# Perceiver block on one core: buffers and loads of the output weights, the order of a split product, and the columns of a score row

## The chip, the cores and the metric

The kernel runs on one core of a Trainium2 chip. The metric is the device time of one execution in microseconds (us); lower is better. TensorE (PE in the profile, with PEld for its weight loads) does the matmuls, VectorE (DVE), ScalarE (ACT) and GpSimd (POOL) the element-wise work, and every DMA of this kernel is issued by SyncE (SP). A partition is one of the 128 rows of the on-chip memory.

## The reference, cut to what matters

There are 8 batches with 64 query rows of width 512 and a context of 1601 rows of width 512. Five blocks follow each other, each on a layer norm and with a residual:

```python
x = x + xattn0(ln(x), ctx)   # 32 heads of 128, 8 key/value heads; Wq, Wkv, Wo with biases
x = x + mamba(ln(x))         # 1024 channels, 16 states, 64 steps: conv, silu, softplus, scan, gate, W_out
x = x + ffn0(ln(x))          # ternary 512 x 512 weight and a bias
x = x + xattn1(ln(x), ctx)   # softmax(x ctx^T) ctx, no weights
x = x + attn1(ln(x))         # causal, 32 heads of 16, rotary; wq, wk, wv, wo
x = x + ffn1(ln(x))          # octonion ternary, gated: 512 -> 1360 -> 512
```

Here `ln` is the layer norm. Everything is fp32, and the result is wanted nearly at fp32. The rest of the names below follow this list: "the main attention" is xattn0, which is most of the arithmetic, and "the second cross attention" is xattn1.

## The kernel before, in words

**Two streams.** The main attention is one stream, `x_all` (L517): 64 units, one for each batch and key/value head, and in each unit six steps that interleave the keys (L363), values (L334), scores (L385), the products with the values (L464) and, for each odd batch, the output product with Wo (`x_wo`, L492 to 515, into the tile `w_ps`, added at L514). The other five blocks are "side chains", one for each pair of batches (a group; groups 0 to 3 are batches 0-1, 2-3, 4-5 and 6-7). A side chain (L761) can begin when both its batches have their rows of xattn0; it is a generator that goes through `mamba` (L789), `ffn`, `xattn1` (L997), `attn1` (L1106) and `ffn1`. Two more generators run at the beginning: `halves` (L606) and `prep` (L620, which makes the ternary weights).

**What sets the order.** `run` (L1285) takes one piece of the main stream after the other, and after each piece lets the side generators go on until they have yielded the cost that is due by then (`advance`, L1314; the goal is linear from a chain's start over its SPAN, L1367: 3.1 main batches for groups 0 and 1, 2.6 for group 2). In this way the program is written in one order. The instructions of the side chains on VectorE, ScalarE and GpSimd are kept in that order (L55 to 76, `keep_in_program_order`); those of TensorE and the DMA issues of SyncE are placed by the scheduler, which lays all engines out on a time line and takes a buffer when it is free. So a side chain that waits for a buffer on that line is placed later, and so are the pinned pieces behind it.

**The tail.** Behind the last unit the main stream is flushed (the rest of the last unit and its Wo product). Then the pools of the main stream are closed, new ones with other sizes opened (L47, `BUFS_TAIL`), the pinning is off, and group 3's chain goes through in the form for the tail (`tail=True`): weights as pairs of 4 KB a partition, 12 buffers for `w2`. What is left of group 2's chain is interleaved behind it and takes the tags w2 and b4 from the tail's pool (REST, L1374: 8 and 3 buffers).

**Precise products.** Where fp32 accuracy is wanted at the faster fp32r rate, a number is split into a high part that fp32r holds exactly and a low part, the rest. A product is then three matmuls, high by high, high by low and low by high (`mm3`, L742). `halves` makes the two parts of Wo (32 tiles of 128 x 512), W_outT (8 tiles) and the four matrices of attn1 (16 tiles) once, in the beginning, and stores them to DRAM (`wo_s`, `wout_s`, `wat_s`): it loads a tile (L614), splits it by a ScalarE copy and a GpSimd subtraction (L616, L105 and 106), and stores both parts (L617). It uses the tag `wo` with three buffers, the same that `x_wo` uses later for its weights (L507).

**Buffers of the change.** A tag is a ring of buffers, and L46 (`BUFS`) gives their number before the tail. `lv` holds tiles of 4 KB a partition, three of them: u (L793), dt (L847) and dus = dt times u (L865) of the mamba block. `w2` holds tiles of 2 KB, three of them: the weights of every `mm3` outside the tail, so that the two parts of a weight take two buffers and come in two DMAs (L753 to 755). W_out is read in `mamba_out` (L968), which splits the gated output and calls `mm3` once for each of eight chunks; this comes behind the scan of all chunks (L949 to 952), and the gates (L958, with projections at L801) stand between. The keys' weights of the main stream have a tag of their own, `wk`, with one buffer; `wo` is as large.

**The second cross attention.** For each of the two batches, `scores` (L1005) loads ctxT in pieces of up to 256 columns (L1018), multiplies (L1021: the row of 512 is split over two halves of the array, so four matmuls a piece), adds the halves (L1032, L1034), and takes the maximum, the exponential and the sum by tiles. Outside the tail the 1601 columns lie in three tiles S of 512, 512 and 577 columns; the third is filled from two accumulators, 384 and 194 columns. `values` (L1051) transposes the weights in 13 blocks (L1059), loads ctxN (L1072, L1074) and multiplies (L1077).

Of the kernel before, what the change touches and what calls it, by code (L numbers as in the profile page):

```python
# [16 lines left out]
P = 128  # L17
# [28 lines left out]
BUFS = {"a2": 5, "lv": 3, "bc": 1, "xpad": 1, "b2": 5, "b4": 2, "w2": 3, "xr": 2}  # L46
# [32 lines left out]
class Kernel:  # L79
# [412 lines left out]
    def x_wo(self, b, i):  # L492
# [13 lines left out]
        for g in range(G):  # L506
            w = self.sb("wo", [P, 2, D], FR, pool=self.xp, bufs=WOB)  # L507
            nc.sync.dma_start(out=w.bitcast(FP), in_=self.wo_s[i][:, g])
            parts = ((0, 0), (0, 1), (1, 0))
            for a, m in parts:  # L510
                nc.tensor.matmul(ps, lhsT=ot[:, a, g].rearrange("p b t -> p (b t)"), rhs=w[:, m], start=k == 0, stop=k == len(parts) * G - 1)  # L511
                k += 1
            yield 0.64
# [92 lines left out]
    def halves(self):  # L606

        nc, i = self.nc, self.i
        todo = [(i["Wo"][k * G + g], self.wo_s[k][:, g]) for k in range(NKV) for g in range(G)]
        todo += [(i["W_outT"][h], self.wout_s[h]) for h in range(NCH)]  # L610
        todo += [(i["attnT"][m, c], self.wat_s[m][c]) for m in range(4) for c in range(NC)]
        for src, dst in todo:
            t = self.sb("wo", [P, 2, D], FR, pool=self.xp, bufs=WOB)
            nc.sync.dma_start(out=t[:, 1].bitcast(FP), in_=src)  # L614
            yield 0.5
            self.split(t[:, 0], t[:, 1], t[:, 1].bitcast(FP), eng=nc.gpsimd)  # L616
            nc.sync.dma_start(out=dst, in_=t.bitcast(FP))  # L617
            yield 0.5
# [123 lines left out]
    def mm3(self, ps, lhsT, wt, N, start, stop, exact=False, tg="w2"):  # L742
# [5 lines left out]
        elif self.tail:  # L748
# [7 lines left out]
        nc.tensor.matmul(ps, lhsT=lhsT(0), rhs=wh, start=start, stop=False)  # L756
        if not exact:
            nc.tensor.matmul(ps, lhsT=lhsT(0), rhs=wl, start=False, stop=False)
        nc.tensor.matmul(ps, lhsT=lhsT(1), rhs=wh, start=False, stop=stop)  # L759
# [29 lines left out]
    def mamba(self, gi, x, xo):  # L789
# [3 lines left out]
        u = self.sb(self.tv, [P, NCH, 2, T])  # L793
# [174 lines left out]
    def mamba_out(self, c, uc, ps):  # L968
        yt = self.sb("a2", [P, 2, P], FR)
        self.split(yt[:, 0, :], yt[:, 1, :], uc.rearrange("p b t -> p (b t)"))  # L970
        self.mm3(ps, lambda a: yt[:, a, :], self.wout_s[c], D, c == 0, c == NCH - 1, tg=self.t4)
# [25 lines left out]
    def xattn1(self, bs, x, xo):  # L997
# [3 lines left out]
        GW = [(0, (256, 256)), (1, (256, 256)), (2, (192, 192)), (2, (194,))]  # L1001
        SW = [512, 512, 577]
        TS = ((0, 4), (4, 8), (8, NT))

        def scores(k, b):  # L1005
            q0 = k * T
            if self.tail:
                s = self.sb("bc", [T, LP])
                S = [s[:, :512], s[:, 512:1024], s[:, 1024:]]
            else:  # L1010
                S = [self.sb("b2", [T, 512]), self.sb("b2", [T, 512]), self.sb("b2", [T, 578])]
# [26 lines left out]
            nm = self.sb("s1m", [T, 4])  # L1038
            for m in range(3):
                nc.vector.tensor_reduce(nm[:, m : m + 1], S[m][:, : SW[m]], AX.X, ALU.max)  # L1040
            nc.vector.tensor_reduce(nm[:, 3:4], nm[:, 0:3], AX.X, ALU.max, negate=True)
            sm2 = self.sb("s1s", [T, 4])
            for m in range(3):
                nc.scalar.activation(S[m][:, : SW[m]], S[m][:, : SW[m]], AF.Exp, bias=nm[:, 3:4], accum_out=sm2[:, m : m + 1])
            sm = sm2[:, 3:4]
            nc.vector.tensor_reduce(sm, sm2[:, 0:3], AX.X, ALU.add)
# [4 lines left out]
        def values(k, b, S, sm):  # L1051
            q0 = k * T
            pts = []
            for m, (t0, t1) in enumerate(TS):
                pt = self.sb("b2", [P, 5, T])
                tp = self.acc().rearrange("p (t q) -> p t q", q=T)
                for t in range(t0, t1):
                    r = rows_of(t)
                    nc.tensor.transpose(tp[:r, t - t0, :], S[m][:, (t - t0) * P : (t - t0) * P + r], self.ident[:T, :T])  # L1059
# [312 lines left out]
MAMBA_TAGS = ("a2", "lv", "bc", "xpad", "sm")  # L1372
# [117 lines left out]
```

## Time and profile before

| what | value |
|---|---|
| runs | 2690.39, 2688.52 and 2685.12 us; median 2688.52 |
| the profiled execution | 2687.19 us |
| span of its profile (first to last instruction on the core) | 2685.1 us |
| mean granted clock of TensorE over the span | 0.983 |
| matmul records | 16,320 |
| DMA issues on SyncE | 1,331 |
| bytes moved | 466 MB, 174 GB/s over the span |
| last add of the main attention (`w_ps`, L514) begins | 2385.5 us |

Times in the views below are microseconds from the start of the span, and "busy" is the time in which an engine executed instructions. The table by stretches gives for each engine the busy time and, in brackets, the number of instructions in the stretch, then the clock that TensorE was granted (1.00 is full speed), the mean busy share of the sixteen DMA engines, and what they moved. The same table can be made for the instructions of one line alone; the first figure pair is then PE and the second PEld. The view of waits gives, for an engine, what it was about to do, what ended its wait, and the total, number and longest of these waits in us.

When the blocks of the groups ran in this execution (us):

| group | mamba | xattn1 | attn1 | ffn1 |
|---|---|---|---|---|
| 0 | 671-1125 | 1137-1268 | 1338-1425 | 1495-1577 |
| 1 | 1218, gates to 1734 | 1792-1922 | 1970-2094 | 2153-2232 |
| 2 | 1870-2375 | 2402-2510 | from 2539 | to 2650 |
| 3 (in the tail) | 2388-2532 | 2547-2592 | 2597-2645 | to 2685 |

### The profile page before, as it was taken

The page shows a single profiled execution, that of the slowest core. Times are in us where ns is not written, and L with a number is a line of the kernel's source. Part 1 is how long each engine was busy: PE and PEld are TensorE (multiplying, and loading weights), DVE is VectorE, ACT ScalarE, POOL GpSimd, SP SyncE. Part 2 cuts the span into 40 slices and gives each one's busy share as a digit, 9 for nine tenths or more (in the row PEclk, how much of TensorE's full clock was granted, in tenths as well). Part 3 has the DMA queues.
Part 4 walks back from the last instruction along what each step waited for, and adds up shares of the span by engine and source line. Part 5 has one row for each costly group of instructions (what it writes and reads, how often), then busy time and mean ns, then how long its engine had stood idle before and what let it go on. Part 6 is the DMA issues. An engine that isn't in the chain of part 4 may idle for free.

```text
span 2685.1 us, 43976 instructions
## 1 busy us (share of the span) xinstructions
PE 2549.7 (95%) x16320; PEld 2269.3 (85%) x16320; DVE 1667.6 (62%) x2739; ACT 1350.2 (50%) x3128; POOL 1247.6 (46%) x1243
## 2 busy tenths in 40 slices
PE   7999999999999999999999999999999999977797
PEld 6988999999999899978989988988898898964544
DVE  4534357665687775545567676554657777668754
ACT  4545454344556554544555554544546545436433
POOL 2434463463368663521367457521239556405420
PEclk9999999999999999999999999999999999987899
DMA  9788876675213244764324452665343455466674
GB/s 308 225 295 276 281 239 190 203 240 180 67 66 105 68 133 150 232 190 145 97 98 148 149 161 89 216 201 164 102 135 92 137 159 155 143 226 216 234 261 166
DMA packets 311126, 466.08 MB, mean 174 GB/s; under 512 B 88440, under 2 KB 187768, under 8 KB 306432
## 3 DMA queue, kind: packets, MB, share of 16 engines
q1 hardware_dynamic: 310912, 463.28, 53.4%
q8 instruction: 128, 2.10, 0.3%
q14 instruction: 86, 0.70, 0.1%
HBM read 389.66 MB, written 73.53 MB: 173 GB/s over the span
## 4 chain that ended last, share of the span: by engine, by line
PE 68%; DMA 9%; DVE 9%; POOL 7%; issue 4%; ACT 3%; SPq 0%; POOLq 0%; DVEq 0%; ACTq 0%
PE v_ps L334 16%; PE k_ps L363 16%; PE o_ps L464 10%; PE s_ps L385 8%; POOL a L65 3%; PE w_ps L511 2%; PE acc L274 2%; DVE a L65 2%; PE acc L1077 2%; PE acc L801 2%; PE acc L1021 1%; PE acc L759 1%; PE acc L756 1%; POOL ss L452 1%; DMA b<-in_ctxT_dram 1%
## 5 line engine op out<-in xcount | busy, mean ns | idle before, releaser
L363 PE MATMUL k_ps<-cxb,wk 128*128 128x384 f32 x2304 | 470.3, 347 | 35.3 <-DVE mx L392 13.2
L334 PE MATMUL v_ps<-wv,cxb 128*128 128x256 f32 x3456 | 467.9, 281 | 1.0 <-DVE kt L109 0.6
L334 PEld LDWEIGHTS v_ps<-wv,cxb 128*128 128x128 f32 x3456 | 438.0, 188 | 19.3 <-issue 11.7
L363 PEld LDWEIGHTS k_ps<-cxb,wk 128*128 128x128 f32 x2304 | 405.3, 191 | 53.2 <-DVE mx L392 15.6
L464 PE MATMUL o_ps<-S,v 128*128 128x256 f32 (+1 forms) x1664 | 413.6, 381 | 7.4 <-DVE rw L479 4.0
L385 PE MATMUL s_ps<-q,kt 128*128 128x256 f32 (+1 forms) x2496 | 413.7, 299 | 5.2 <-DVE mx L392 2.4
L385 PEld LDWEIGHTS s_ps<-q,kt 128*128 128x128 f32 (+1 forms) x2496 | 342.8, 185 | 28.5 <-issue 6.9
L388 ACT COPY S<-s_ps 128x512 f32<-128x512 f32 (+1 forms) x448 | 241.9, 553 | 241.0 <-PE s_ps L385 236.6
L452 POOL TENSOR_TENSOR ss<-ss,S 128x512 f32<-128x512 f32 x254 | 349.3, 1375 | 14.7 <-ACT S L427 1.3
L392 DVE TENSOR_TENSOR mx<-s_ps,mx 128x512 f32<-128x512 f32 x256 | 175.1, 684 | 264.0 <-ACT S L388 262.7
L464 PEld LDWEIGHTS o_ps<-S,v 128*128 128x128 f32 (+1 forms) x1664 | 298.6, 190 | 46.7 <-issue 5.2
L429 POOL TENSOR_TENSOR ss<-S,S 128x512 f32<-128x512 f32 x64 | 84.5, 1320 | 469.4 <-ACT S L427 469.1
L108 ACT ACTIVATE kt<-k_ps,c_bk 128x384 fp32r<-128x384 f32 (+1 forms) x256 | 152.0, 594 | 246.9 <-PE k_ps L363 245.9
L426 DVE TENSOR_TENSOR S<-S,m_ps 128x512 f32<-128x512 f32 (+1 forms) x448 | 257.3, 640 | 20.5 <-PE m_ps L412 20.2
L427 ACT ACTIVATE S<-S 128x512 f32<-128x512 f32 (+1 forms) x448 | 246.7, 599 | 43.4 <-DVE S L426 42.7
L109 DVE SCALAR_TENSOR_TENSOR kt<-k_ps,c_bk,kt 128x384 fp32r<-128x384 f32 (+1 forms) x256 | 160.9, 629 | 158.0 <-ACT kt L108 156.5
L337 ACT COPY v<-v_ps 128x256 f32<-128x256 f32 (+1 forms) x416 | 152.5, 368 | 198.4 <-PE v_ps L334 196.0
L334 PE MATMUL v_ps<-wv,cxt 128*128 128x256 f32 (+1 forms) x1536 | 206.5, 282 | 1.5 <-DVE mx L392 1.0
L334 PEld LDWEIGHTS v_ps<-wv,cxt 128*128 128x128 f32 (+1 forms) x1536 | 192.7, 175 | 10.5 <-issue 3.4
L65 DVE TENSOR_TENSOR_SCAN a<-a,a 128x512 f32<-128x512 f32 x96 | 154.7, 1613 | 62.9 <-POOL a L65 62.8
L363 PE MATMUL k_ps<-cxt,wk 128*128 128x450 f32 x768 | 178.6, 375 | 1.4 <-DVE mx L392 1.3
L65 POOL TENSOR_TENSOR a<-a,bc 128x512 f32<-128x512 f32 x96 | 128.1, 1335 | 90.7 <-DVE a L65 90.7
(357 smaller groups left out, 3947.8 us busy)
## 6 DMA issues: line engine op xcount, KB each, us to landing
wo<-d_wo SPq DMA_DIRECT2D x128, 512.0 KB, 5.3
wk<-d_wk SPq DMA_DIRECT2D x63, 512.0 KB, 3.5
wv<-d_wv SPq DMA_DIRECT2D x31, 1024.0 KB, 5.7
cst<-in_ctxT_dram SPq DMA_DIRECT2D x96, 192.0 KB, 3.0
b<-in_ctxN_dram SPq DMA_DIRECT2D x36, 512.0 KB, 3.7
d_q<-q_t SPq DMA_DIRECT2D x32, 512.0 KB, 5.9
q<-d_q SPq DMA_DIRECT2D x64, 256.0 KB, 3.1
d_wo<-wo SPq DMA_DIRECT2D x32, 512.0 KB, 5.7
```

The costliest lines, as they stand in the source:

```text
L65: return lambda *a, **k: self.tc.keep_in_program_order(f(*a, **k))
L109: eng.scalar_tensor_tensor(lo, src, bias, hi.bitcast(FP), ALU.add, ALU.subtract)
L334: nc.tensor.matmul(ps[:r], lhsT=cx[:, a, c, o : o + r], rhs=w[:, m, c, :], start=k == 0, stop=k == 11)
L337: nc.scalar.copy(vt[:r], ps[:r])
L363: nc.tensor.matmul(ps[:, :wd], lhsT=w[:, a, c, :], rhs=cx[:, m, c, :], start=k == 0, stop=k == 11)
L385: nc.tensor.matmul(sp[:r, gi, :], lhsT=kt[:, a, o : o + r], rhs=q[:, m, :], start=k == 0, stop=k == 2)
L388: nc.scalar.copy(s[:r, :n], sp[:r, :n])
L392: nc.vector.tensor_tensor(mx, sp, S[0] if len(S) == 1 else mx, ALU.max)
L426: nc.vector.tensor_tensor(sv, sv, ps[:r, 1:2].to_broadcast([r, w, 256]), ALU.add)
L427: nc.scalar.activation(sv, sv, AF.Exp, scale=ISC)
L452: nc.gpsimd.tensor_tensor(ss, ss, S[n], ALU.add)
L464: nc.tensor.matmul(ps[:, 0], lhsT=self.v[(b, j, t)][:r, hc : hc + P], rhs=S[t // 2][:r, t % 2], start=t == 0, stop=t == NT - 1)
```

## The change

Six edits, all outside the form of the tail except the third:

1. `lv` has two buffers and not three, and u gets a tag of its own, `lu`, with one: the same room in other rings. `w2` has four buffers and not three (2 KB a partition more).
2. `mamba_out` outside the tail loads the two parts of a W_out chunk as one tile of 4 KB a partition (512 KB in one DMA) from the tag `lv`, where dt and dus lay, and no longer as two from `w2`. That is 24 DMAs fewer in the three groups (1331 to 1307).
3. `mm3` multiplies high by high, low activation by high weight, high activation by low weight; the last two were the other way round.
4. `halves` has two loads ahead of the split, and issues the load of tile k+2 behind the store of tile k.
5. `scores` outside the tail lays the 1601 columns out as 512, 512, 512 and 66 (65 of them used), each from one accumulator; the small tile has a tag `s1x`. Each batch so has one more maximum and one more exponential.
6. The very last quarter of Wo (batch 7, head 7, g = 3) is loaded into the tag `wk`, and not into the fourth use of a ring of three.

```diff
--- before.py
+++ after.py
@@ -43,7 +43,7 @@
 CPLAN = (0, 1, 2, None, None, 3)
 AVPLAN = ((), (), (0, 1, 2, 3), (4, 5, 6, 7), (8, 9, 10, 11), (12,))
 EXPLAN = ((0,), (1, 2), (3,), (4, 5), (6,), ())
-BUFS = {"a2": 5, "lv": 3, "bc": 1, "xpad": 1, "b2": 5, "b4": 2, "w2": 3, "xr": 2}
+BUFS = {"a2": 5, "lv": 2, "lu": 1, "bc": 1, "xpad": 1, "b2": 5, "b4": 2, "w2": 4, "xr": 2}
 BUFS_TAIL = {"a2": 6, "du": 2, "bc": 2, "xpad": 4, "s4": 11, "kb": 3, "b2": 8, "b4": 3, "w2": 12, "xr": 2}
 
 
@@ -504,7 +504,8 @@
         ps = self.px.tile([P, D], FP, name=self.nm("w_ps"), tag="kv", bufs=KVB)
         k = 0
         for g in range(G):
-            w = self.sb("wo", [P, 2, D], FR, pool=self.xp, bufs=WOB)
+            last = (b, i, g) == (self.B - 1, NKV - 1, WOB)
+            w = self.sb("wk" if last else "wo", [P, 2, D], FR, pool=self.xp, bufs=1 if last else WOB)
             nc.sync.dma_start(out=w.bitcast(FP), in_=self.wo_s[i][:, g])
             parts = ((0, 0), (0, 1), (1, 0))
             for a, m in parts:
@@ -609,12 +610,22 @@
         todo = [(i["Wo"][k * G + g], self.wo_s[k][:, g]) for k in range(NKV) for g in range(G)]
         todo += [(i["W_outT"][h], self.wout_s[h]) for h in range(NCH)]
         todo += [(i["attnT"][m, c], self.wat_s[m][c]) for m in range(4) for c in range(NC)]
-        for src, dst in todo:
-            t = self.sb("wo", [P, 2, D], FR, pool=self.xp, bufs=WOB)
-            nc.sync.dma_start(out=t[:, 1].bitcast(FP), in_=src)
+        ts = {}
+
+        def load(k):
+            if k < len(todo):
+                ts[k] = self.sb("wo", [P, 2, D], FR, pool=self.xp, bufs=WOB)
+                nc.sync.dma_start(out=ts[k][:, 1].bitcast(FP), in_=todo[k][0])
+
+        load(0)
+        load(1)
+        yield 1
+        for k, (src, dst) in enumerate(todo):
+            t = ts.pop(k)
+            self.split(t[:, 0], t[:, 1], t[:, 1].bitcast(FP), eng=nc.gpsimd)
             yield 0.5
-            self.split(t[:, 0], t[:, 1], t[:, 1].bitcast(FP), eng=nc.gpsimd)
             nc.sync.dma_start(out=dst, in_=t.bitcast(FP))
+            load(k + 2)
             yield 0.5
 
     def prep(self):
@@ -739,13 +750,13 @@
         self.nc.sync.dma_start(out=w, in_=wt)
         self.nc.tensor.matmul(ps, lhsT=x, rhs=w, start=start, stop=stop)
 
-    def mm3(self, ps, lhsT, wt, N, start, stop, exact=False, tg="w2"):
+    def mm3(self, ps, lhsT, wt, N, start, stop, exact=False, tg="w2", pair=False):
 
         nc = self.nc
         if exact:
             wh = self.sb(tg, [P, D], FR)[:, :N]
             nc.sync.dma_start(out=wh.bitcast(FP), in_=wt)
-        elif self.tail:
+        elif self.tail or pair:
             w = self.sb(tg, [P, 2, D], FR)
             nc.sync.dma_start(out=w.bitcast(FP), in_=wt)
             wh, wl = w[:, 0], w[:, 1]
@@ -754,9 +765,9 @@
             nc.sync.dma_start(out=wh.bitcast(FP), in_=wt[:, 0])
             nc.sync.dma_start(out=wl.bitcast(FP), in_=wt[:, 1])
         nc.tensor.matmul(ps, lhsT=lhsT(0), rhs=wh, start=start, stop=False)
+        nc.tensor.matmul(ps, lhsT=lhsT(1), rhs=wh, start=False, stop=stop and exact)
         if not exact:
-            nc.tensor.matmul(ps, lhsT=lhsT(0), rhs=wl, start=False, stop=False)
-        nc.tensor.matmul(ps, lhsT=lhsT(1), rhs=wh, start=False, stop=stop)
+            nc.tensor.matmul(ps, lhsT=lhsT(0), rhs=wl, start=False, stop=stop)
 
     def chain(self, gi, bs):
         nc, i = self.nc, self.i
@@ -790,7 +801,7 @@
         nc, i = self.nc, self.i
         tail = self.tail
         lt = self.lnT(x, P, hl=False, tg="a2")
-        u = self.sb(self.tv, [P, NCH, 2, T])
+        u = self.sb(self.tv if tail else "lu", [P, NCH, 2, T])
         gs = 2 if tail else 4
 
         def proj(m):
@@ -968,7 +979,7 @@
     def mamba_out(self, c, uc, ps):
         yt = self.sb("a2", [P, 2, P], FR)
         self.split(yt[:, 0, :], yt[:, 1, :], uc.rearrange("p b t -> p (b t)"))
-        self.mm3(ps, lambda a: yt[:, a, :], self.wout_s[c], D, c == 0, c == NCH - 1, tg=self.t4)
+        self.mm3(ps, lambda a: yt[:, a, :], self.wout_s[c], D, c == 0, c == NCH - 1, tg=self.tv if not self.tail else self.t4, pair=True)
 
     def softplus(self, x, shape, eng):
 
@@ -998,8 +1009,13 @@
 
         nc, i = self.nc, self.i
         lt = self.lnT(x, P, hl=False)
-        GW = [(0, (256, 256)), (1, (256, 256)), (2, (192, 192)), (2, (194,))]
-        SW = [512, 512, 577]
+        if self.tail:
+            GW = [(0, (256, 256)), (1, (256, 256)), (2, (192, 192)), (2, (194,))]
+            SW = [512, 512, 577]
+        else:
+            GW = [(0, (256, 256)), (1, (256, 256)), (2, (256, 256)), (3, (66,))]
+            SW = [512, 512, 512, 65]
+        NS = len(SW)
         TS = ((0, 4), (4, 8), (8, NT))
 
         def scores(k, b):
@@ -1008,7 +1024,7 @@
                 s = self.sb("bc", [T, LP])
                 S = [s[:, :512], s[:, 512:1024], s[:, 1024:]]
             else:
-                S = [self.sb("b2", [T, 512]), self.sb("b2", [T, 512]), self.sb("b2", [T, 578])]
+                S = [*(self.sb("b2", [T, 512]) for _ in range(3)), self.sb("s1x", [T, 66], bufs=1)]
             o = 0
             for m, ws in GW:
                 ps = self.acc()
@@ -1035,15 +1051,15 @@
                 o += e
                 if not self.tail:
                     yield 2 * len(ws)
-            nm = self.sb("s1m", [T, 4])
-            for m in range(3):
+            nm = self.sb("s1m", [T, 5])
+            for m in range(NS):
                 nc.vector.tensor_reduce(nm[:, m : m + 1], S[m][:, : SW[m]], AX.X, ALU.max)
-            nc.vector.tensor_reduce(nm[:, 3:4], nm[:, 0:3], AX.X, ALU.max, negate=True)
-            sm2 = self.sb("s1s", [T, 4])
-            for m in range(3):
-                nc.scalar.activation(S[m][:, : SW[m]], S[m][:, : SW[m]], AF.Exp, bias=nm[:, 3:4], accum_out=sm2[:, m : m + 1])
-            sm = sm2[:, 3:4]
-            nc.vector.tensor_reduce(sm, sm2[:, 0:3], AX.X, ALU.add)
+            nc.vector.tensor_reduce(nm[:, 4:5], nm[:, 0:NS], AX.X, ALU.max, negate=True)
+            sm2 = self.sb("s1s", [T, 5])
+            for m in range(NS):
+                nc.scalar.activation(S[m][:, : SW[m]], S[m][:, : SW[m]], AF.Exp, bias=nm[:, 4:5], accum_out=sm2[:, m : m + 1])
+            sm = sm2[:, 4:5]
+            nc.vector.tensor_reduce(sm, sm2[:, 0:NS], AX.X, ALU.add)
             nc.vector.reciprocal(sm, sm)
             yield 3
             return S, sm
@@ -1056,7 +1072,8 @@
                 tp = self.acc().rearrange("p (t q) -> p t q", q=T)
                 for t in range(t0, t1):
                     r = rows_of(t)
-                    nc.tensor.transpose(tp[:r, t - t0, :], S[m][:, (t - t0) * P : (t - t0) * P + r], self.ident[:T, :T])
+                    src = S[3][:, :r] if t == 12 and len(S) > 3 else S[m][:, (t - t0) * P : (t - t0) * P + r]
+                    nc.tensor.transpose(tp[:r, t - t0, :], src, self.ident[:T, :T])
                 e = min(t1, 12) - t0
                 nc.scalar.copy(pt[:, :e, :], tp[:, :e, :])
                 if t1 == NT:
@@ -1369,7 +1386,7 @@
 HALVES_START = 0.1
 HALVES_END = 0.97
 HALVES_COST = 56.0
-MAMBA_TAGS = ("a2", "lv", "bc", "xpad", "sm")
+MAMBA_TAGS = ("a2", "lv", "lu", "bc", "xpad", "sm")
 FFN_TAIL = (("l", 0), ("l", 1), ("a", 0), ("l", 2), ("a", 1), ("d", 0), ("a", 2), ("d", 1), ("d", 2))
 REST = {"w2":8,"b4":3}
 OTB = 1
```

`self.tv` is `lv` outside the tail and `s4` in it, `self.t4` is `w2` and `s4`.

## The prediction

> **What bounds the kernel now.** I read the page's totals first, then a table of five stretches that I cut at visible marks: the attention; its flush; and the three parts of the tail, split where the last group's scan begins (2441 us, first L941) and ends (2530 us).
>
> ```profile
> PE 2549.7 (95%) x16320; PEld 2269.3 (85%) x16320; DVE 1667.6 (62%) x2739; ACT 1350.2 (50%) x3128; POOL 1247.6 (46%) x1243
> ...
> core 0: us, PE busy (x) PEld busy (x) DVE busy (x) ACT busy (x) POOL busy (x), PEclk, DMA share, GB/s
> 67.00:2345.00 2278.00, 2226.55 (x14556) 2047.17 (x14556) 1415.77 (x2281) 1163.77 (x2668) 1134.48 (x1118) 1.00 0.51 162
> 2345.00:2385.00 40.00, 33.00 (x172) 27.40 (x171) 23.42 (x48) 14.44 (x33) 5.26 (x7) 0.96 0.54 173
> 2385.00:2441.00 56.00, 38.98 (x251) 30.54 (x249) 34.62 (x101) 30.02 (x91) 2.44 (x11) 0.75 0.87 292
> 2441.00:2530.00 89.00, 68.62 (x396) 46.61 (x394) 82.78 (x113) 52.95 (x157) 61.57 (x61) 0.85 0.54 178
> 2530.00:2686.00 156.00, 131.48 (x683) 74.36 (x683) 78.50 (x155) 56.77 (x124) 24.54 (x25) 0.96 0.67 233
> ```
>
> Up to 2345 us TensorE is busy 2226.55 of 2278 us: whatever matmul is put there lengthens it, and only 51.5 us could be won. The tail is another regime: part A (56 us) has DMA at 0.87 and a clock of 0.75; part B (89 us) has VectorE busy 82.78 us, 93%, so the scan sets it; part C (156 us) has TensorE at 84%. Next, who TensorE waits for. The weights that the change is about are small entries:
>
> ```profile
> PE k_ps L363 <- DMA wk<-d_wk: 9.2, 5, 4.1
> ...
> PE acc L758 <- DMA w<-d_wout: 3.2, 2, 2.2
> ...
> PE w_ps L511 <- DMA wo<-d_wo: 3.0, 4, 1.2
> ...
> PE acc L758 <- DMA w<-d_wat: 1.7, 2, 1.0
> ```
>
> The columns are us in total, times, longest: 17.1 us in all; no more than that can come from the weights' waits directly.
>
> **What the change does to the order.** The two programs' instruction orders, laid side by side, show the moves. The main attention's 12,496 matmuls are the same. The side chain of group 2 (batches 4 and 5) stands about 540 main matmuls earlier by its gate (L801); group 1's is 220 to 580 earlier from its gate on; group 0's up to its gate is unmoved. I read this as a queue effect: side work is in program order on VectorE, ScalarE and GpSimd, so a chain that waits for a w2 tile holds back the next chain's scan; with a fourth tile and 4 KB W_out pairs it holds it less. What counts is the end: before, group 2's feed-forward block and whole second cross attention stand behind the last main matmul; after, 119 of these matmuls stand ahead of it (56 of L1021, 25 of L1077, 26 of L1059, 8 exact ones, 4 of L709). The tail begins with group 2's self-attention.
>
> **Part by part.** *Attention: +33.* The moved matmuls cost what the same lines cost in the attention (each fp32 L1021 and L1077 matmul is two records):
>
> ```profile
> 67.00:2345.00 2278.00, 27.38 (x224) 13.76 (x224) 1.00 0.51 162
> 67.00:2345.00 2278.00, 29.30 (x104) 5.86 (x104) 1.00 0.51 162
> 67.00:2345.00 2278.00, 5.32 (x52) 3.95 (x52) 1.00 0.51 162
> ```
>
> These are the busy us of L1021, L1077 and L1059 in the first stretch. 112 x 0.122 = 13.7; 50 x 0.282 = 14.1; 26 x 0.102 = 2.7; eight matmuls of 512 columns at 0.23 (start to start in the run from 2603.9 us) 1.9; one L709 group 0.6: 33.0 us. Nothing hides it, as TensorE is at 98%.
>
> *Halves: -4.* The five waits of L363 for wk all lie between 147 and 317 us, in the halves' time; there SP waits 68.4 us for d_wo stores before loads (L614) and 41.9 us for GpSimd before stores (L617), with the wk loads queued behind. Loads two ahead fill these waits, and several wk loads now stand ahead of a store they stood behind. The new wait (a load for the store of the tile before last) holds SP, and so wk, q, wv. Bounds: all 9.2 gone, or 5 more (one SP wait for a wo split is up to 7.1); I take -4.
>
> *W_out in pairs, fourth w2 tile: -4.* d_wout 3.2 and d_wat 1.7, less a remnant. The first pair now waits for the scan's last exp (it reads dt); queued behind it on SP are W_inT loads. A 512 KB pair lands in 3.8 us in the tail, a 256 KB half in 4.1, and 24 issues of 0.33 us go away on a queue that is not the bound. Bounds -5 to +4 (one pair wholly exposed).
>
> *Last quarter of Wo in wk's tile:* the 0.8 us at 2383.8, counted in the next item. *Low half first:* the low activation is wanted one matmul (0.23) earlier, the low weight later; some six waits on each side, so within 1.4 either way; I take 0. *Scores in 512+512+512+66:* same columns; per batch one more Exp (0.3 to 0.76, by L118 and the 577-wide Exp) and one more reduction (0.14 to 0.74), on engines 50 and 62% busy: 0, and 1 to 3 in the flush if exposed. The 66-column load lies between 0 and the 4.6 of the 388 KB load; prefetched, 0.
>
> *Flush: -3.* 7.0 of its 40 us are idle: 3.2 for d_wout (already counted), 3.0 for L108, 0.8 for wo. The cross attention's matmuls now fill such holes, but its softmax stands between the last scores and the first values (8.2 us in the tail of before, 2431.6 to 2439.8) and shares VectorE with the last unit's maximum: bounds -4 to +6.
>
> So group 3's chain starts 33 - 4 - 4 - 3 = **22 us later**.
>
> *Tail A: 0.* Gone: waits of L1021 for ctxT, which held L835 (2.3), ScalarE (2.6), and its Exps ahead of L984 (2.3). New: 24 w2_r loads of 256 KB and group 2's L1133, which waits for VectorE, between group 3's L829; and six attnT loads now stand ahead of the bc loads, 1.5 MB, 5 us at 292 GB/s. Bounds -7 to +8.
>
> *Tail B: +9.* I summed VectorE's instructions between the first and last L938 in both orders, each at its median in this trace. Group 2's softmax pieces (6.2) go; its self-attention's L1176, L1177, L1178 and L1180 at about 0.7, splits and a layer norm (14.8) come: +8.6 on an engine at 93%. GpSimd gets 10 us (L1159, L1182) but is at 69%. Bounds +3 to +14.
>
> *Tail C: -24.* Group 2's work leaves group 3's path: in its cross attention 6 of 43 us (L1163, 12 of the L756 kind between L1021); in its self-attention 4 (16 matmuls, 2603.3 to 2607.4), 4 (group 2's SiLU ahead of L1130), 5 (2625.5 to 2630.5), 2 (2637.3 to 2639.2); before L1244 3 (2646.8 to 2650.6); 5 smaller: 29, less 5 for group 2's feed-forward pieces that now stand there. Bounds -11 (matmuls alone) to -35.
>
> Tail: 0 + 9 - 24 = -15. **Sum 22 - 15 = +7.** The profiled execution took 2687.2 (span 2685.1 and 2.1 around it): 2694.2; the median of the runs, 2688.5, is 1.3 above it: **2695**.
>
> *A rule against the change.* The trace's clock is 1.00 in the attention, 0.75 in A and 0.85 in B, and L1021 costs 0.148 a record in A (8.31 for 56) against 0.122. The Trainium skill, "TensorE: Matmul & The Clock Gate", Part 1, agrees on the cause: after an idle window of some 3.4 us the array runs at half rate until it is busy again. By the rule a tail with 33 us less TensorE work is throttled more, an estimated 2 to 4 us more in A and B; by the rows alone B hangs on VectorE and gains nothing from the clock. The sum goes without it.
>
> **Rivals.** *1, faster (2664 to 2676).* The tail was slow because of group 2's cross attention. For: L1021, L1077 and L1059 of group 2 hold TensorE 8.31 + 7.84 + 1.21 + 17.60 + 2.17 + 1.43 = 38.6 us in A and B, and TensorE waits 7.6 + 4.6 + 3.8 in the tail for their loads and Exps. If the path sheds the 38.6 and half of the 16: -47 + 22 = -25, 2664. Against: B's 93% of VectorE. *2, slower (2713).* The scan decides: group 2's self-attention in VectorE's order hands to ScalarE and GpSimd and back, and every hand-over stalls the scans queued behind: B +14, and C gives only 11: 22 + 14 - 11 = +25. It decides once B is above some 100 us. *3, an even exchange (2686).* The 20 us that TensorE waits for VectorE in the scan stretches (L363 <- mx 14.4, and smaller ones) are spaces that earlier side matmuls fill: start +12, tail -15: -3. That the weights' waits stay (the change does not do what it says) costs 8 and lies inside my range.
>
> **Chances.** Forecast 0.42 (2688 to 2703), rival 1 0.24, rival 2 0.20, rival 3 0.14. A measurement can tell about 0.2%, 5.4 us, from none: faster is below 2683.1, slower above 2693.9. The forecast gives slower 0.25, same 0.17; rival 1 faster 0.24; rival 2 slower 0.20; rival 3 same 0.09, faster 0.05. Together faster 0.29, same 0.26, slower 0.45. The forecast's own range is 2688 to 2703; to hold eight in ten it must reach into both rivals: 2664 to 2714.
>
> **What would show it.** The last w_ps add about 22 us later; no L1021 of group 2 behind it; the stretch between first and last L941 near 98 us with VectorE above 90%; from there to the end near 132; no wait of TensorE for d_wout; at most 6 us for wk. Wrong if the scan stretch does not grow, or if the attention ends less than 10 us later.

## The result, and the profile after

The changed kernel takes 2730.35 us (median of 4 runs, 2725.69 to 2733.40), the kernel before 2687.38 (4 runs): ratio 1.0159, 95% interval 1.0141 to 1.0176. It is 43 us slower, where 7 were forecast, and lies outside the range. The profiled execution took 2731.97 with a span of 2730.2, against 2687.19 and 2685.1.

From here on the tail is cut at three marks of the trace: the start of the last Wo add (end of the attention), the first and the last matmul of group 3's scan (L941 before, L952 after). A lies between the first two, B is the scan, C runs from the scan's end to the end of the span. The last add begins at 2384.8 us before; 2385.5, which the table ahead of the prediction gives, is its end. The prediction's own A and B meet at 2441 us; that is where VectorE begins the scan (first L935, 2441.0; L946 at 2480.9 after), and not the first L941, which begins at 2452.0. Cut at that mark, A changes by -3.7 and B by +12.6, so the row of the forecast can be compared.

| kernel | attention ends | A | B | C | tail |
|---|---|---|---|---|---|
| before | 2384.8 | 67.2 | 77.4 | 155.7 | 300.3 |
| forecast | +22 | 0 | +9 | -24 | -15 |
| after | 2428.4 (+43.6) | 63.7 (-3.5) | 89.8 (+12.4) | 148.2 (-7.5) | 301.8 (+1.5) |

So the whole loss stands in the attention, and the tail gave nothing back. The page's first section and the table by stretches of the changed kernel, cut at the attention's last 40 us and at A, B and C:

```profile
PE 2565.8 (94%) x16320; PEld 2285.1 (84%) x16320; DVE 1671.2 (61%) x2745; ACT 1352.7 (50%) x3140; POOL 1237.9 (45%) x1243
```

```profile
67.00:2388.00 2321.00, 2267.76 (x14758) 2071.89 (x14758) 1437.20 (x2325) 1178.62 (x2713) 1127.24 (x1119) 0.99 0.52 165
2388.00:2428.00 40.00, 33.02 (x166) 20.74 (x162) 18.45 (x38) 13.01 (x33) 3.88 (x3) 0.91 0.53 170
2428.00:2492.00 64.00, 39.97 (x222) 31.36 (x220) 44.91 (x108) 33.83 (x101) 16.34 (x25) 0.80 0.89 306
2492.00:2582.00 90.00, 63.94 (x381) 52.53 (x382) 78.32 (x113) 48.01 (x138) 60.71 (x60) 0.76 0.28 87
2582.00:2731.00 149.00, 108.79 (x530) 64.09 (x528) 59.99 (x119) 46.75 (x101) 10.47 (x12) 0.88 0.57 189
```

The kernel before in the same three stretches of its tail:

```profile
2385.00:2452.00 67.00, 42.53 (x259) 31.14 (x257) 45.62 (x113) 34.37 (x105) 12.94 (x20) 0.74 0.81 275
2452.00:2529.00 77.00, 64.68 (x384) 45.81 (x385) 71.15 (x98) 48.60 (x143) 50.92 (x51) 0.87 0.54 174
2529.00:2686.00 157.00, 131.87 (x687) 74.56 (x685) 79.13 (x158) 56.77 (x124) 24.68 (x25) 0.96 0.67 233
```

TensorE is the first figure pair behind the length. In the tail it is busy 26.4 us less (212.7 against 239.1, the sums of the three lines), yet the three stretches last 303 us against 301: the idle time of TensorE in them grew from 62 to 90. That the second cross attention of group 2 really left the tail is seen in the score line alone (L1037 after; PE, then PEld):

```profile
2388.00:2428.00 40.00, 3.37 (x32) 1.51 (x28) 0.91 0.53 170
2428.00:2492.00 64.00, 0.00 (x0) 0.00 (x0) 0.80 0.89 306
2492.00:2582.00 90.00, 0.00 (x0) 0.00 (x0) 0.76 0.28 87
2582.00:2731.00 149.00, 14.00 (x112) 9.15 (x112) 0.88 0.57 189
```

Ahead of 2582 us there is no such record in the tail; the 112 in C are group 3's own.

To see where the 43.6 us of the attention come from, I gave every moment up to the last Wo add to a matmul of the main stream, to a side matmul, or to idle time of TensorE (a moment in which two overlap goes to the one that began first), and took the difference to before: **side +34.3, main +8.7, idle +0.5**. Given to the one that began later, the overlap makes it +31.4 and +11.6, so the parting of these two is good to about 3 us. The score line alone took 40.9 us ahead of the tail (L1037) against 27.4 (L1021 before): +13.5, where 13.7 was summed. The main stream has the same matmuls; they took longer. The idle time is as long, but with other causes. The waits of TensorE between the ninth and the last Wo add (from 943 us before, from 938 after), before and then after (us in total, times, longest):

```profile
PE k_ps L363 <- DVE mx L392: 12.1, 6, 4.2
PE acc L758 <- DMA w<-d_wout: 3.2, 2, 2.2
PE w_ps L511 <- ACT ot L108: 3.0, 1, 3.0
PE m_ps L412 <- DVE mc L405: 3.0, 3, 2.1
...
PE acc L758 <- DMA w<-d_wat: 1.7, 2, 1.0
...
PE acc L756 <- DMA w<-d_wout: 0.2, 1, 0.2
```

```profile
PE m_ps L403 <- DVE mx L395: 5.5, 3, 3.5
PE k_ps L363 <- DVE kt L109: 5.3, 3, 2.7
PE k_ps L363 <- DVE mx L392: 4.3, 4, 2.2
PE s_ps L385 <- DVE mx L392: 3.8, 3, 2.7
PE acc L720 <- DVE b L65: 3.8, 2, 3.5
PE acc L767 <- DMA w<-d_wat: 2.6, 1, 2.6
...
PE acc L767 <- DMA lv<-d_wout: 0.4, 1, 0.4
```

The wait for d_wout went from 3.4 to 0.4 (L756 and L758 before, L767 after), as the pairs should make it; that for d_wat, which has no pairs outside the tail, grew from 1.7 to 2.6. All waits that VectorE ends grew from 24.4 to 33.5 us.

### The profile page after: what moved, and what is told of

Same layout as the page of the kernel before. It is cut to its first block, busy times and chain, and to the rows that moved or that the text cites. A ratio compares the mean times of both kernels' runs of the same rounds, so it can differ in the third digit from the quotient of the medians.

```text
span 2730.2 us, 43990 instructions
## 1 busy us (share of the span) xinstructions
PE 2565.8 (94%) x16320; PEld 2285.1 (84%) x16320; DVE 1671.2 (61%) x2745; ACT 1352.7 (50%) x3140; POOL 1237.9 (45%) x1243
## 4 chain that ended last, share of the span: by engine, by line
PE 71%; DVE 9%; DMA 7%; POOL 7%; issue 4%; ACT 3%; SPq 0%; POOLq 0%; DVEq 0%; ACTq 0%
PE k_ps L363 16%; PE v_ps L334 16%; PE o_ps L464 10%; PE s_ps L385 8%; PE w_ps L512 3%; POOL a L65 2%; DVE a L65 2%; PE acc L274 2%; PE acc L812 2%; PE acc L1094 2%; PE acc L1037 2%; PE acc L767 2%; POOL ss L452 2%; PE acc L768 2%; DMA cst<-in_ctxT_dram 1%
## 5 line engine op out<-in xcount | busy, mean ns | idle before, releaser
L363 PE MATMUL k_ps<-cxb,wk 128*128 128x384 f32 x2304 | 473.3, 349 | 26.0 <-ACT cxb L105 10.1
L363 PEld LDWEIGHTS k_ps<-cxb,wk 128*128 128x128 f32 x2304 | 405.4, 192 | 46.5 <-ACT cxb L105 10.5
L108 ACT ACTIVATE kt<-k_ps,c_bk 128x384 fp32r<-128x384 f32 (+1 forms) x256 | 151.7, 592 | 220.1 <-PE k_ps L363 219.4
L65 ACT ACTIVATE a<-lv,c_A_log 128x128 f32<-128x128 f32 x384 | 122.8, 392 | 99.9 <-DVE a L65 99.8
```

What stands on the lines that cost most here:

```text
L65: return lambda *a, **k: self.tc.keep_in_program_order(f(*a, **k))
L363: nc.tensor.matmul(ps[:, :wd], lhsT=w[:, a, c, :], rhs=cx[:, m, c, :], start=k == 0, stop=k == 11)
```

## The experiments

Every kernel was timed against the kernel before on the same chip; there are four chips, and the medians of before on them are 2687.5 to 2689.1 us. "Attention ends" and "tail" are from one profiled execution, to be set beside 2384.8 and 300.3. One execution is not the median: e2's profiled one is 6.7 us above its median, e8's 4.6 above, e14's 4.7 below, and 19 executions of before alone reach from 2679.6 to 2695.0. So differences of a few us between two rows of the last two columns say nothing by themselves.

| run | kernel | median us | ratio, 95% interval | attention ends | tail |
|---|---|---|---|---|---|
| e1 | after, group 2 held back | 2693.11 | 1.0020 (1.0006 to 1.0035) | 2392.4 | 298.5 |
| e2 | before + score tiles + fourth w2 | 2739.65 | 1.0192 (1.0171 to 1.0213) | 2447.8 | 296.4 |
| e3 | after, three w2 tiles | 2694.52 | 1.0023 (1.0012 to 1.0034) | 2398.8 | 292.1 |
| e4 | before + halves | 2674.54 | 0.9943 (0.9925 to 0.9962) | 2374.1 | 299.5 |
| e5 | e4, group 2 ends before xattn1 | 2650.79 | 0.9860 (0.9829 to 0.9891) | 2380.2 | 267.3 |
| e6 | e4 without group 2's xattn1 | 2675.56 | 0.9956 (0.9944 to 0.9968) | 2379.3 | 296.6 |
| e7 | e4 + W_out pairs | 2691.28 | 1.0015 (1.0002 to 1.0028) | 2385.1 | 302.3 |
| e8 | e4 + order of the products | 2704.14 | 1.0061 (1.0039 to 1.0083) | 2405.5 | 301.3 |
| e9 | e4, SPAN of group 1 at 3.0 | 2708.94 | 1.0074 (1.0058 to 1.0091) | 2389.2 | 321.4 |
| e10 | e4, SPAN of group 1 at 3.2 | 2701.03 | 1.0049 (1.0037 to 1.0061) | 2390.2 | 311.2 |
| e11 | e4 + score tiles + wk tile | 2678.78 | 0.9961 (0.9948 to 0.9974) | 2374.9 | 302.1 |
| e12 | e8, group 2 held back | 2705.79 | 1.0067 (1.0050 to 1.0084) | 2397.6 | 302.4 |
| e13 | e4, group 2 ends behind xattn1 | 2658.58 | 0.9882 (0.9862 to 0.9902) | 2376.0 | 279.3 |
| e14 | after, group 2 ends behind xattn1 | 2694.60 | 1.0026 (1.0013 to 1.0040) | 2423.3 | 264.3 |
| e15 | e4, group 2's rest due earlier in the tail | 2682.28 | 0.9967 (0.9955 to 0.9978) | 2380.3 | 300.1 |
| e16 | e4, group 2's rest due later in the tail | 2685.41 | 0.9988 (0.9977 to 0.9999) | 2382.2 | 303.8 |

The theory, F for filling: the second cross attention of group 2 was nearly free in the tail, where TensorE had holes; in the attention TensorE is full, and it costs its whole length.

### Does the moved work make the loss? (e1, e6)

e1 is the changed kernel in which group 2's chain may not pass the end of its feed-forward block before the tail opens (`cap` is 194 of the chain's 377 for group 2, 0 for the others):

```diff
             while c["got"] < goal:     # in advance(), ahead of it:
+                if c["cap"] and not self.flush and not base["tail"]:
+                    goal = min(goal, c["cap"])
```

> The changed kernel, but group 2's side chain may not go beyond its feed-forward block until the tail opens; all 112 L1037-type score matmuls, 26 transposes and 52 value records of its second cross attention then stand behind the last main matmul again. Theory F (filling: these 34 us of TensorE work were free in the holes of the tail and cost their full length in the attention): the last w_ps add comes 34 us earlier than in the changed kernel, near 2394, the tail stays near 300, the time is 2690 (2683 to 2700). Rival W (the wider rings themselves, with the chains standing earlier on VectorE and slower main matmuls, cost the time): the attention keeps at least 20 of its 44 us, and the time is 2710 or more.

2693.11: 37 of the 43 us are gone, with every edit still in. The attention ends at 2392.4, 36.0 us earlier than in the changed kernel: 29.8 of side matmuls, 4.1 of main, 2.1 of idle time. The tail is 298.5. F is borne out and W, which wanted 2710 or more, is not.

e6 takes the work away instead of moving it (the kernel is the one before with the halves, e4):

```diff
+        if gi == 2:
+            def skip(x, xo):
+                nc.vector.tensor_copy(xo, x)
+                for _ in range(19):
+                    yield 4
+            blocks[2] = skip
         for f in blocks[: LAST_STAGE - 1]:
```

> The kernel before with the pipelined halves, and group 2's second cross attention left out (a copy takes its place; its cost in the interleaving is kept). Theory F: these 38 us of TensorE work cost nothing or little in the tail: 2664 to 2675 against 2674.5 with them. Rival S: 2636 to 2650.

2675.56 against 2674.54 in e4: nothing is won by leaving it out. This is the most direct reading of the study: the lines of this block hold TensorE for 38.6 us in the tail of before; without them TensorE's busy time in the tail falls by 24.2 us (238.4 to 214.2), and the tail by 2.9 (299.5 to 296.6). S is refuted. The other matmuls of the tail so took some 14 us more; the granted clock was lower there (the tables are below).

### Which edit moves it? (e2, e3, e4, e7, e8, e11, e12)

e2 is the kernel before with the new score tiles, which free the room, and `"w2": 4` for `"w2": 3`; e3 is the changed kernel with `"w2": 3`.

> The kernel before with two edits alone: the 512+512+512+66 score tiles (which free the room) and the fourth w2 tile. No pairs, old halves, old order of the three matmuls, no wk tile. The order then has 108 instead of 216 of xattn1's matmuls of group 2 and 3 behind the last main matmul, as in the changed kernel. Theory F: this alone makes the loss, and without the 5 us of the halves: 2735 (2726 to 2742). Rival P (the pairs in lv, which wait for the scan, and the order of the three matmuls make it): below 2700.

> The changed kernel with three w2 tiles instead of four, all else kept. 200 of xattn1's matmuls stand behind the last main matmul (216 before, 109 in the changed kernel). Theory F: nearly all of the loss is gone, 2688 (2680 to 2698). Rival P (pairs and matmul order): 2715 or more.

Both as F has it: the fourth tile with the score tiles gives 2739.65 (the score tiles by themselves add little, see e11), and without the tile the changed kernel falls to 2694.52. Neither the pairs nor the order of the products is needed for the loss.

e4 is the kernel before with `halves` alone taken from the changed one (edit 4):

> The kernel before with the pipelined halves alone; the order of TensorE's side work behind the last main matmul is unchanged. In the changed kernel the first w_ps add came 5.0 us earlier (425.2 against 430.2) with 5.6 us less idle time of TensorE. If that is kept to the end: 2683 (2680 to 2685). Rival: what is won at 430 us is a wait moved to the next stall, as the main stream is at 98 per cent and later gaps are set by other engines: 2687 to 2690.

2674.54, below the range that was expected, and the only edit that gains clearly. The waits of TensorE before the first Wo add (430.2 us before, 420.6 here) show why; first before, then e4:

```profile
PE k_ps L363 <- ACT cxb L105: 10.4, 2, 10.1
PE k_ps L363 <- DMA wk<-d_wk: 9.2, 5, 4.1
PE acc L274 <- DVE q_t L109: 1.3, 1, 1.3
```

```profile
PE k_ps L363 <- ACT cxb L105: 10.7, 2, 10.4
PE s_ps L385 <- DMA q<-d_q: 1.3, 1, 1.3
PE k_ps L363 <- ACT S L388: 1.3, 1, 1.3
...
PE k_ps L363 <- DMA wk<-d_wk: 0.4, 1, 0.4
```

Of the five waits for wk, 9.2 us, one of 0.4 is left, and what was won at 420 us is still there at the end of the attention (10.7). Not all of the 14 us is sure to be the edit's: e5, e6, e13, e15 and e16 have the same order of side and main matmuls in the attention, and end it at 2376.0 to 2382.2, so 2.6 to 10.7 us ahead of before. Why the same order varies by 8 us stays open; with one profiled execution each, it can't be told from the spread of one kernel's own executions.

e7 adds edits 1 and 2 to e4 (without the fourth w2 tile), e8 edit 3, and e12 is e8 with the cap of e1. e11 adds edits 5 and 6.

> The kernel before with the pipelined halves and the W_out pairs (u in a tag of its own, pairs in lv). Behind the last main matmul 12 matmuls of group 2 are gone (4 transposes, 8 of the feed-forward), xattn1's 216 are unmoved. Theory F, a price by the matmuls that move ahead of the end (8 at 0.23 and a transpose group): 2674.5 + 3 - 3 for the d_wout waits = 2675 (2670 to 2680). Rival Q: the pair's first load waits for the scan that reads dt and stalls the weights queued behind it on SyncE; this is the other part of the 18 us that separate the capped kernel from the halves alone: 2685 or more.

> The kernel before with the pipelined halves and the new order of the three matmuls (low activation by high weight second). 57 matmuls of group 2 move ahead of the last main matmul (45 of xattn1, 8 of the feed-forward, 4 transposes). Theory F, a price by the matmuls moved: 45 at 0.15 to 0.28 and 3 us, less what the tail sheds (nothing): 2684 (2680 to 2690). Rival N: the order of two matmuls in one group costs nothing, 2674 to 2678.

> The kernel with the pipelined halves and the new order of the three matmuls (2704), with group 2's chain held at the end of its feed-forward block until the tail opens: xattn1's 45 matmuls go back behind the last main matmul. Theory F: 13 us come back, 2691 (2686 to 2696); what is left above 2674.5 is idle time in the attention. Rival N2 (the whole 30 us are the new order's own price, as the tail waits longer for the last product): 2700 or more.

> The kernel before with the three edits that let nothing of group 2 pass the end of the attention: pipelined halves, score tiles of 512+512+512+66, and the last quarter of Wo in wk's tile. Group 1's gates stand 88 main matmuls later. By the prediction's terms the score tiles cost 0 to 3 in the flush and wk saves 0.8: 2674 (2670 to 2679). Theory R: the 88 may cost as a placebo does, 2680 to 2690.

The pairs cost 17 us, the order of the products 30, though only 12 and 57 side matmuls pass the end; F's price by matmuls moved (about 3 and 10 us) misses both by far, and N, that the order costs nothing, is refuted. The size of Q's forecast is right, its mechanism is not: TensorE waits 1.8 us for the pairs, and for DMAs in all 4.6 us against 4.9 in e4, but the waits for VectorE grow to 33.3 us, from 22.9 in e4 (both from the ninth to the last Wo add). In e8 it is 32.4, and waits for DMAs go from 4.9 to 14.3. e12 is a miss for F: in the profiles, holding group 2 back takes 10.0 us of side matmuls out of the attention while idle time grows by 4.6, and the median of 2705.79 is no better than 2704.14. N2's number holds, its reason doesn't: the tail is 2.9 us longer than in e4, the attention 23.5. So there is a second cost, which isn't a price per matmul. e11 stays near e4 (2678.78): score tiles and wk tile are no part of it.

### Is the second cost the edits' own? (e9, e10)

Two placebos are e4 (edit 4 and no other) with only the second entry of SPAN changed, the length over which group 1's chain is spread, to 3.0 and 3.2 from 3.1:

> The kernel before with the pipelined halves, and no other edit than the third... group 1's SPAN at 3.0 instead of 3.1: a placebo that only shifts the side chains (group 1's gates 175 main matmuls earlier, group 2's 62 later; 10 more side matmuls behind the last main one, none fewer). Theory R (any other interleaving of the side chains brings TensorE new waits for VectorE in the attention, so the 10 us of idle time in the kernels with pairs or with the new matmul order are not the price of these edits): 2680 to 2695, with 5 to 15 us more idle time of TensorE in the attention than the halves alone. Rival E (the edits themselves cost it): 2672 to 2677.

> The same placebo the other way: group 1's SPAN at 3.2. Group 1's gates stand 78 main matmuls earlier by the scheduler's choice, group 2's 19 later, nothing else passes the end. Theory R: 2680 to 2695. Rival E: 2672 to 2677.

2708.94 and 2701.03: 34 and 26 us above e4 with no edit of buffers, loads or products at all. So R holds in its direction, and a re-interleaving by itself costs as much as the pairs or the order of the products did. Its size was underrated, and half of it stands where R had not put it: the attention ends 15 to 16 us later (9.6 and 14.0 of it idle time), and the tails are 22 and 12 us longer. R's mechanism isn't shown: the waits for VectorE are 24.2 and 27.9 here, nearly as in e4, those for DMAs 10.0 and 10.5 (4.9 in e4). What makes the interleaving before a lucky one stays open. What the runs show is that of five others tried around it four were worse by 17 to 34 us (e7 to e10), and one, with group 1's gates 88 main matmuls later, by 4 (e11).

### What does the tail pay for? (e5, e13, e14, e15, e16)

If the cross attention cost the tail only 3 us, what does it pay for? e5 cuts group 2's chain off behind the feed-forward block, e13 and e14 behind the second cross attention:

```diff
+        if gi == 2:
+            blocks = blocks[:2]     # e5; blocks[:3] in e13 and e14
         for f in blocks[: LAST_STAGE - 1]:
```

> The kernel before with the pipelined halves, and group 2's side chain cut off behind its feed-forward block: its second cross attention, self-attention and gated feed-forward are left out (the rows of batches 4 and 5 in the output are those of the feed-forward block). The tail then holds group 3 alone. With group 2 it is 299.5 us long from the last w_ps add. Theory F (the tail is set by group 3's own chain, and group 2's work only fills its holes): 270 to 295 us of tail are left. Rival S (the tail is a sum of work; group 2 has about 38 + 38 + 20 us of TensorE work there): about 205 us.

> The kernel before with the pipelined halves, and group 2 cut off behind its second cross attention, which stays in the tail (self-attention and gated feed-forward of batches 4 and 5 are left out). The tail is 299.5 us with all of group 2, 296.6 without its cross attention, 267.3 with group 3 alone. Theory T (the tail pays for group 2's self-attention and feed-forward, about 29 us, and its cross attention is free): tail 268 to 274, time 2645 to 2652. Rival U (group 2's blocks overlap in what they cost, any of them alone holds the tail): tail 285 or more.

> The changed kernel with the same cut: group 2 ends with its cross attention, most of which runs ahead of the last main matmul (self-attention and gated feed-forward of batches 4 and 5 are left out). Attention as in the changed kernel, near 2428. Theory T: tail 265 to 272, so the changed kernel's tail pays 30 us or more for the same two blocks, and time near 2698. Rival U: the tail stays within 10 us of 302.

| what of group 2 is in the tail | run | A | B | C | tail |
|---|---|---|---|---|---|
| cross attention, self-attention, gated feed-forward | e4 | 66.5 | 77.5 | 155.5 | 299.5 |
| self-attention, feed-forward | e6 | 61.1 | 86.6 | 148.9 | 296.6 |
| the same, changed kernel | after | 63.7 | 89.8 | 148.2 | 301.8 |
| cross attention | e13 | 64.3 | 79.1 | 135.9 | 279.3 |
| nothing | e5 | 60.7 | 71.3 | 135.3 | 267.3 |
| little of the cross attention, changed kernel | e14 | 58.1 | 70.7 | 135.5 | 264.3 |

F's reading is right for e5, though its 270 was still too high: group 3 alone takes 267 us, where S wanted 205, and the 67.1 us by which group 2 raises TensorE's busy time in the tail (171.3 to 238.4) add only 32. T is right for e14 (264.3; 265 to 272 was expected) and not quite for e13 (279.3; 274 at most was expected, U wanted 285 or more): the cross attention costs 12.0 us where the two other blocks are missing (e13 less e5), and 2.9 where they are there (e4 less e6). The two blocks that stay cost 20.2 us while the cross attention is there (e4 less e13), 29.3 when it is left out (e6 less e5), and 37.5 in the changed kernel (after less e14). That is where much of the expected gain of the tail went: from e4 to e6, A and C get 5.4 and 6.6 us shorter, and B gets 9.1 longer. **With the cross attention gone, group 2's self-attention moves up into the scan**, on the engine that is fullest there. The table by stretches for A, B and C of e4 and of e6, and for B and C of e14:

```profile
2374.00:2441.00 67.00, 41.78 (x262) 30.07 (x261) 45.69 (x114) 34.64 (x107) 13.02 (x20) 0.76 0.82 275
2441.00:2518.00 77.00, 64.78 (x386) 45.80 (x385) 70.91 (x97) 48.21 (x142) 50.84 (x51) 0.88 0.54 175
2518.00:2674.00 156.00, 131.84 (x684) 74.36 (x683) 79.02 (x157) 56.79 (x124) 24.66 (x25) 0.96 0.68 234
```

```profile
2379.00:2440.00 61.00, 43.81 (x231) 31.50 (x229) 46.43 (x114) 33.27 (x99) 17.94 (x26) 0.84 0.95 323
2440.00:2527.00 87.00, 61.55 (x395) 50.32 (x396) 82.13 (x112) 50.69 (x144) 60.53 (x59) 0.77 0.30 104
2527.00:2676.00 149.00, 108.88 (x511) 62.45 (x509) 55.48 (x113) 43.29 (x95) 10.42 (x12) 0.84 0.55 182
```

```profile
2481.00:2552.00 71.00, 44.38 (x275) 40.48 (x276) 63.98 (x82) 43.62 (x127) 51.51 (x52) 0.78 0.22 71
2552.00:2688.00 136.00, 96.27 (x446) 50.97 (x445) 48.01 (x99) 36.38 (x82) 10.33 (x11) 0.82 0.50 163
```

VectorE (third pair) is busy 63.98 of 71 us in the scan of e14, with group 3 alone, 70.91 of 77 in e4, 82.13 of 87 in e6 and 78.32 of 90 in the changed kernel. It is the fullest engine each time, and TensorE is busy for less time in the longer stretch of e6 than in that of e4. That VectorE sets the stretch is argued from this. What is new on it in the changed kernel's B are the softmax lines of group 2's self-attention (groups of VectorE, busy time and mean ns):

```profile
L1195 DVE TENSOR_TENSOR b<-b,a1m 128x512 f32<-128x512 f32 x4 | 4.3, 1084 | 0.0
...
L1197 DVE TENSOR_REDUCE a1m<-b 128x8 f32<-128x512 f32 x4 | 2.7, 670 | 0.1
...
L1193 DVE SCALAR_TENSOR_TENSOR b<-acc,c_causal 128x512 f32<-128x512 f32 x3 | 2.0, 673 | 0.0
L1194 DVE TENSOR_REDUCE a1m<-b 128x8 f32<-128x512 f32 x3 | 2.0, 671 | 0.0
```

e15 and e16 change only when group 2's rest is due once the tail is open (end 8.25 and 9.2 instead of 8.6):

> The kernel before with the pipelined halves; only from the opening of the tail on, what is left of group 2 is due earlier (end 8.25 instead of 8.6), so it stands further forward in the order between group 3's pieces. The attention is unchanged. Theory T (self-attention and feed-forward of group 2 stand on group 3's path where they are interleaved with it): 2675 to 2690, the tail up to 15 us longer, most of it in the scan stretch. Rival: no change, as the scheduler fills holes anyway, 2672 to 2677.

> The same the other way: group 2's rest is due later (end 9.2), so its self-attention and feed-forward stand behind group 3's last piece in the order and only fill holes. Theory T: the tail sheds part of the 29 us, 2655 to 2672. Rival V (group 2's own chain, 3 blocks in a row, then ends last): 2680 or more.

Tails of 300.1 and 303.8 against 299.5: earlier changes nothing, later costs 4 us. T's hope that the two blocks could be pushed into holes fails. V's number holds, its reason doesn't: in e16 the last add of group 2 (L1289) begins at 2677.2 us, that of group 3 at 2682.3. The 8 and 11 us by which the medians lie above e4 are mostly the attention's own spread (2380.3 and 2382.2).

## Why the prediction was wrong

**Right: the move and its price.** The order of the instructions was read rightly, and the 33.0 us for the moved matmuls were measured as 34.3 (31.4 with the overlap given the other way).

**Right: A and B.** A came out at -3.5, within its bounds, and B at +12.4 (forecast +9, bounds 3 to 14), in the main for the reason given, self-attention on VectorE during the scan: its busy time in B grew by 7.2 us (71.15 to 78.32; 8.6 was summed), and the other 5 us are idle time of VectorE.

**Right in the mechanism: halves.** -4 was forecast; the changed kernel's first Wo add came 5.0 us earlier, and the halves alone give 2.6 to 10.7 at the end of the attention.

**Failed: "Tail C: -24".** It measured -7.5, outside its bounds. I had added up 29 us in which group 2 held TensorE or stood ahead of group 3 in C, and gave 5 back for the feed-forward block. All of group 2 costs C 20 us (155.5 in e4 less 135.3 in e5), its cross attention next to nothing of that (135.9 in e13), and what stays of group 2 in the changed kernel's C, the gated feed-forward, keeps 13 (148.2 less 135.5 in e14). Occupied time was taken for time on the path, in a stage where TensorE was shown at 84%. In the trace of after the serial pieces of group 2 stand beside group 3's: at 2595.6 us TensorE ends a wait of 7.7 us for group 2's SiLU, whose pieces alternate on VectorE with group 3's layer norm, and at 2650.0 another of 5.3.

**Failed: "weights -4" and "flush -3".** The attention ended 21.6 us later than summed. Of these, 11.5 are idle time: -11 was forecast for the halves, the weights and the flush together, and +0.5 was measured. The waits for d_wout went as forecast (3.4 to 0.4), those for d_wat did not (1.7 to 2.6), and the idle time of the attention stayed (+0.5, and +6.1 without the 5.6 that the halves won by the first Wo add), as waits for VectorE grew by 9.1 us. The flush is the same picture: 33.02 busy of 40 us as before, with 3.5 for L403 and 2.5 for ctxN in place of d_wout and L108. A stall was taken off the sum without a price for what the new order would bring. e7 to e10 show that this price can be large, 17 to 34 us for a different interleaving, and e1, with all edits and no moved cross attention, still stands 18.6 us above e4. Why a given interleaving costs what it does stays open.

**Missing: the main stream's matmuls, +8.7.** The prediction has no term for them. The clock is 1.00 in the attention before, 0.99 after, and 0.91 against 0.96 in the flush; the direction fits, but the rounding (0.01 of 2321 us is 23 us) is too coarse to say how much of the 8.7 that is. In the tail the clock of B fell from 0.87 to 0.76 as TensorE work left it. The rule weighed in the prediction, that the array runs at half rate after an idle window (the Trainium skill, "TensorE: Matmul & The Clock Gate", Part 1), agrees with that row. The prediction looked for its price in A and B alone. In C the clock fell too, from 0.96 to 0.84 in e6 and 0.88 in the changed kernel, and group 3's own matmuls there got slower: the 48 of one line of its gated feed-forward are busy for 10.1 us in e4 (L1254), 12.0 in e6 (L1262) and 11.5 in the changed kernel (L1261), the longest 404 ns against 792. So a part of what leaving out the cross attention should win may have been taken back by slower matmuls. How large it is isn't shown: no run leaves out the work and keeps the clock.

**The rivals.** Rival 2 came nearest, in its point and in B: the scan stretch in the prediction's own cut, from VectorE's first work for the scan at 2481 us to 2582, is 101 us long (89 before), above the 100 from which it was to decide, with VectorE busy 89.32 of it (88%, where over 90 was named). Its 2713 was too low mostly because the attention ended 21.6 us later than it was summed. Rival 1, that the tail sheds the 38.6 us and more, is refuted by e6. Rival 3, that earlier matmuls fill spaces of TensorE in the attention, had the start 12 us later, and it was 43.6. Of the signs named, the one on L1021 came as told, "the last w_ps add 22 us later" was 44, and "near 132 to the end" was 148. Neither of the two signs of being wrong came, as the scan stretch grew and the attention ended more than 10 us later; the length of C, where the tail failed, was not among them.

The fastest version that computes everything is e4, the halves alone, at 0.9943 of before; no complete version built on it was faster.

## What to carry to other kernels

Work that fills holes can cost little where it stands (2.9 us of tail for 38.6 us of TensorE here) and its full length where it is moved to: before a block is counted as a gain for the stage that it leaves, leave it out there and see whether the stage gets shorter. In a stage where one engine is at 90%, ask what moves up into the freed place and which engine it needs. And when more buffer room lets a scheduler run side work earlier, it changes the whole interleaving: compare it with placebo shifts of the same order before its effect is put down to the edit.

## What the runs showed that was not expected

Taking a 38.6 us block of TensorE work out of the tail changed the time by 1 us (e6). A tenth in one entry of SPAN, with the same instructions, cost 26 to 34 us (e9, e10), as much as the order of the products (30) and more than the pairs (17); only the fourth w2 tile cost more. Six kernels with the same order of matmuls in the attention ended it 8 us apart, in one execution each.
